# The neighbour sums of layer 3 as seven products of half matrices

## The chip, the cores and the metric

The kernel runs on one core of a Trainium2 chip. The core has five engines with a queue each: TensorE (PE in the profile, with its weight loads as PEld), VectorE (DVE), ScalarE (ACT), GpSimd (POOL) and SyncE (SP, which issues most DMAs here). Each queue is worked off in order. The metric is the device time of one execution in microseconds (us), lower is better. It is given as the median of a few runs.

## The reference

A stack of four graph layers over 16 graphs (batches) of 1024 nodes with 256 features each. The change lies in the last layer alone. With `h` the normalised and rectified input of one batch (1024 x 256) and `adj` its 1024 x 1024 adjacency matrix, layer 3 computes:

```python
h = jnp.maximum(_layernorm(x, axis=-1), 0.0)
neighbor_sum = jnp.einsum('bnm,bmd->bnd', adjacency, h)
agg = epsilon * h + neighbor_sum
h = jnp.einsum('bnd,dh->bnh', agg, W1) + b1        # 256 -> 1024
h = jax.nn.silu(_rmsnorm(h, rms_weight))
out = jnp.einsum('bnh,hd->bnd', h, W2) + b2        # 1024 -> 256
x = x + out
```

Everything is fp32. The first three layers, which take the first 3340 us or so of the execution, stay as they are.

## The kernel before

Layer 3 (`layer_3`, from L1093) works through the batches one after another. Matrices lie with 128 rows on the partitions, so `h[b]` is a tile of 8 row blocks by 256 columns, and the transposed adjacency of a batch is held as two halves, `at[b][0]` and `at[b][1]`, each of 8 row blocks by 512 output nodes. The epsilon term is folded in by adding `epsilon` to the diagonal blocks of `at` on GpSimd (`diagonal`, L1151).

One pass of the main loop (L1321) for batch b consists of:

- `load(b + 2)`: DMAs on SyncE for `x`, `hn` (what becomes `h`) and the two halves of `at`. Three halves fit at a time: two in a tile named `bxt`, one in `at`.
- `inner(b)`: `agg` times `W1`, written as seven products of half matrices (Strassen's scheme in Winograd's form) for each of four blocks k of 128 hidden features. Each product is one 128x128 by 128x512 matmul into a PSUM tile named `ph`, of which there are five (`bufs=5`). Per block, ScalarE copies the first product to `p1`; VectorE forms `u2` from the second and `p1`, `u3` from the third and `u2`, and four results `hh` (L1214). ScalarE squares each result into a tile `sq` (L1216), of which there are two, and GpSimd adds it into `ss` (L1218). The last result of a block is put off until after the next block's first product (`left`).
- `sums(b + 1)`: the neighbour sums of the next batch, in four parts, one for each half of the nodes and each half of the features. A part is eight matmuls of 128x128 by 128x512 that accumulate into one `ph`. ScalarE copies each part to `ag`, and four VectorE subtractions (L1195 to L1199) make the combinations `tt` that the next `inner` needs.
- `norm`: `mean` (after part 0) transposes `ss` on TensorE, reduces it on VectorE and takes the power -1/2 on GpSimd; `spread` (after part 1) transposes the result back. Then VectorE multiplies each of 16 tiles of `hh` by it (L1261) and ScalarE applies SiLU (L1262).
- `outer(b)`: `hh` times `W2`, again as seven products, each of 16 matmuls of 128x128 by 128x128 into PSUM tiles named `po`. VectorE makes combinations of `hh` in place (`combine`, L1273), one of them in the tile `s1`.
- `prepare(b + 2)`, called inside `outer` and queued on VectorE behind the update of `x21`: `x + hn`, statistics, the power -1/2 on GpSimd, `shift` (L1171), eight ReLUs on ScalarE that write `h` (L1173), and four GpSimd additions of `b2` (L1177).
- the output DMA, issued from GpSimd (L1337).

The order on each queue isn't the order of the code. It is fixed when the kernel is built, by a planner that goes through its own estimate of the durations and, whenever an engine is free, takes the ready instruction that stands first in the code. Work of later passes is moved forward into gaps in this way. On the chip the queues then run strictly in the order so fixed, whatever the real durations are.

In the profile, an fp32 matmul of the code appears as two MATMUL records, so one part of `sums` shows as 16 records and one product of `inner` as two.

Of the kernel before, what the change touches and what calls it, by code (L numbers as in the profile page):

```python
# [9 lines left out]
F32 = mybir.dt.float32  # L10
AF = mybir.ActivationFunctionType
ALU = mybir.AluOpType
# [4 lines left out]
P = 128  # L17
B, N, D, H = 16, 1024, 256, 1024
NT = N // P
DC = D // P  # L20
# [20 lines left out]
def gnn_stack(ctx: ExitStack, tc: tile.TileContext, a: dict, out: bass.AP):  # L41
    nc = tc.nc
# [29 lines left out]
    def rows(ap):  # L72
        return ap.rearrange("(t p) d -> p t d", p=P)
# [1019 lines left out]
    def layer_3(shared, x, hn, at, h, eye):  # L1093
        with ExitStack() as st:
            wp = st.enter_context(tc.tile_pool(name="w3", bufs=1))
            big = st.enter_context(tc.tile_pool(name="big3", bufs=2))
            small = st.enter_context(tc.tile_pool(name="small3", bufs=2))
            psum = st.enter_context(tc.tile_pool(name="psum3", bufs=2, space=PSUM))
# [14 lines left out]
            NH = 512  # L1113
# [3 lines left out]
            a11, a12, a21, a22 = (w1[:, c, p * HH * P : (p + 1) * HH * P] for p in range(2) for c in range(2))  # L1117
            nc.gpsimd.tensor_tensor(ws[:, 0], a21, a22, ALU.add)
            nc.gpsimd.tensor_tensor(ws[:, 1], ws[:, 0], a11, ALU.subtract)
            nc.gpsimd.tensor_tensor(a21, a11, a21, ALU.subtract)  # L1120
            nc.gpsimd.tensor_tensor(ws[:, 2], a12, ws[:, 1], ALU.subtract)

            wt = wp.tile([P, 3, HH, P], F32, name="wt")
# [6 lines left out]
            def load(b):  # L1130
                if b:
                    x[b] = big.tile([P, NT, D], F32, name="x", bufs=3)
                    nc.sync.dma_start(x[b], rows(x2_d[b]))
                    hn[b] = shared.tile([P, NT, D], F32, name="hb")
                    nc.sync.dma_start(hn[b][:, : NT - 1], rows(hn_d[b])[:, : NT - 1])
                    nc.sync.dma_start(hn[b][:, NT - 1], hs_d[NT - 1][b // GB][b % GB * P : (b % GB + 1) * P])
                    at[b] = []
                while len(at[b]) < N // NH:
                    n0 = NH * len(at[b])

                    if (2 * b + len(at[b])) % 3 < 2:
# [35 lines left out]
                    nc.gpsimd.tensor_tensor(to[:, t : t + 2], x[b][:, t : t + 2], b2[:, None].to_broadcast([P, 2, D]), ALU.add)  # L1177
                x[b] = to

            def sums(b):  # L1180

                ag = big.tile([P, DC, N], F32, name="ag", bufs=1)
                tt = big.tile([P, 4, NH], F32, name="tt", bufs=1)
                b21 = []

                def part(n0, c):
                    pa = psum.tile([P, NH], F32, name="ph", bufs=5)
                    for mt in range(NT):
                        nc.tensor.matmul(pa, h[b][:, mt, c * P : (c + 1) * P], at[b][n0 // NH][:, mt],  # L1189
                                         start=mt == 0, stop=mt == NT - 1)  # L1190
                    nc.scalar.copy(ag[:, c, n0 : n0 + NH], pa)
                    if (n0, c) == (0, 1):
                        b21.append(pa)
                    if (n0, c) == (NH, 0):
                        nc.vector.tensor_sub(tt[:, 0], pa, ag[:, 0, :NH])  # L1195
                    if (n0, c) == (NH, 1):
                        nc.vector.tensor_sub(tt[:, 1], pa, tt[:, 0])
                        nc.vector.tensor_sub(tt[:, 2], pa, ag[:, 0, NH:])
                        nc.vector.tensor_sub(tt[:, 3], b21[0], tt[:, 1])  # L1199
                return (ag, tt), [lambda n0=n0, c=c: part(n0, c) for n0 in range(0, N, NH) for c in range(DC)]  # L1200

            def inner(ag, tt):

                hh = [big.tile([P, HC, NH], F32, name=f"hh{q}", bufs=1) for q in range(2)]
                ss = [small.tile([P, NH], F32, name=f"ss{q}", bufs=1) for q in range(2)]
                begun = [False, False]

                def product(lhsT, rhs, onto=None):
                    ph = onto if onto is not None else psum.tile([P, NH], F32, name="ph", bufs=5)
                    nc.tensor.matmul(ph, lhsT, rhs, start=onto is None, stop=True, skip_group_check=onto is not None)  # L1210
                    return ph

                def result(k, q, ph, u):
                    nc.vector.scalar_tensor_tensor(hh[q][:, k], ph, b1[:, k : k + 1], u, op0=ALU.add, op1=ALU.add)  # L1214
                    sq = small.tile([P, NH], F32, name="sq") if begun[q] else ss[q]
                    nc.scalar.activation(sq, hh[q][:, k], AF.Square)  # L1216
                    if begun[q]:
                        nc.gpsimd.tensor_tensor(ss[q], ss[q], sq, ALU.add)  # L1218
                    begun[q] = True

                left = lambda: None
                for k in range(HH):
                    mine = slice(k * P, (k + 1) * P)
                    p1, u2, u3 = (small.tile([P, NH], F32, name=name) for name in ("p1", "u2", "u3"))
                    ph = product(a11[:, mine], ag[:, 0, :NH])
                    nc.scalar.copy(p1, ph)
                    left()
                    ph = product(ws[:, 1, mine], tt[:, 1])
                    nc.vector.tensor_add(u2, ph, p1)
                    ph = product(a21[:, mine], tt[:, 2])  # L1230
                    nc.vector.tensor_add(u3, ph, u2)
                    p5 = product(ws[:, 0, mine], tt[:, 0])
                    result(HH + k, 1, p5, u3)
                    result(HH + k, 0, product(a22[:, mine], tt[:, 3]), u3)
                    result(k, 0, product(a12[:, mine], ag[:, 1, :NH]), p1)
                    left = lambda k=k, mine=mine, p5=p5, u2=u2: result(
                        k, 1, product(ws[:, 2, mine], ag[:, 1, NH:], p5), u2)
                left()
                return hh, ss

            def norm(hh, ss):

                got = {}

                def mean():
                    all_ = small.tile([P, N // P], F32, name="all")
                    for q in range(2):
                        pq = psum.tile([P, NH // P, P], F32, name="po", bufs=3)
                        for n in range(NH // P):
                            nc.tensor.transpose(pq[:, n], ss[q][:, n * P : (n + 1) * P], ident)  # L1250
# [12 lines left out]
                return mean, spread  # L1263
# [50 lines left out]
            load(0)  # L1314
            prepare(0)
            load(1)
            ags, parts = sums(0)
            for part in parts:
                part()
            prepare(1)  # L1320
            for b in range(B):  # L1321
                if b + 2 < B:
                    load(b + 2)
                hh, ss = inner(*ags)
                mean, spread = norm(hh, ss)
                parts = [lambda: None] * 4
                if b + 1 < B:
                    ags, parts = sums(b + 1)
                parts[0]()
                mean()  # L1330
                parts[1]()
                spread()
                parts[2]()
                parts[3]()

                outer(b, hh, (lambda: prepare(b + 2)) if b + 2 < B else (lambda: None))
                nc.gpsimd.dma_start(rows(out[b]), x[b])  # L1337

    layers_0_1()
    with tc.tile_pool(name="shared", bufs=2) as shared:  # L1340
        x, hn, at, h = {}, {}, {}, {}
# [49 lines left out]
```

## Time and profile before

| what | us |
|---|---|
| runs shown | 4623.85, 4627.27, 4629.18 |
| median | 4627.27 |
| span of the profiled execution | 4622.5 |
| one pass of the main loop of layer 3 (from one `inner` to the next) | 78.31 |
| of it `inner` | 24.04 |
| the two first parts of `sums` with `mean` and `spread`'s transposes | 15.48 |
| the two last parts of `sums` | 13.73 |
| `outer` | 25.06 |

The profile gives the span from the first to the last instruction, and no time of its own beyond it; the median of the runs is 4.8 us above the span. The stage times are from the chain of waits for one pass in the steady part, the one that starts at 3924.34 us. Group rows of the profile list, for each line, engine and operation: the count, the busy time in us with the mean of one instruction in ns, and the idle time of the engine before them with what ended it.

### The profile page before, as it was taken

What the parts mean: (1) busy time and instruction counts of PE and PEld (TensorE: products, weight loads), DVE (VectorE), ACT (ScalarE), POOL (GpSimd) and SP (SyncE); (2) the same over time, 40 slices, a digit from 0 to 9 for tenths busy, and PEclk for the clock granted to TensorE, in tenths of its full rate; (3) what the DMA queues carried; (4) which work ended last, traced back from release to release, by engine and by line L of the source; (5) the groups of instructions that cost most, each with busy time, mean ns of one, the idle gap of its engine ahead of it and who ended that gap; (6) DMA issues with size and microseconds to landing.
All of it is one profiled execution on the core that took longest, in us unless ns stands there. A gap on an engine that the chain in (4) does not pass through costs nothing. (4 is left out here: it accounts for less than half of the span.)

```text
span 4622.5 us, 54868 instructions
## 1 busy us (share of the span) xinstructions
PE 4336.9 (94%) x19223; PEld 2956.2 (64%) x19223; DVE 2535.5 (55%) x6436; ACT 1279.5 (28%) x2741; POOL 1623.5 (35%) x1914
## 2 busy tenths in 40 slices
PE   8999799999997899999999999999799999999998
PEld 4444345555554687778787878787655656565656
DVE  6667944555554344444444444445356666676765
ACT  1111111221121232323232323233234333333333
POOL 3222333433333333332332323234244444445352
PEclk9999899999998999999999999999899999999999
DMA  4333244455544644454444454542142222232310
GB/s 150 112 116 100 73 112 146 164 194 188 156 145 154 196 138 154 131 166 141 154 121 151 131 159 135 167 144 73 55 142 89 100 92 92 88 104 82 110 46 19
DMA packets 530989, 576.78 MB, mean 125 GB/s; under 512 B 42544, under 2 KB 439472, under 8 KB 528304
## 3 DMA queue, kind: packets, MB, share of 16 engines
q1 hardware_dynamic: 499536, 460.27, 32.0%
q0 software_dynamic: 31040, 111.44, 6.9%
q8 instruction: 206, 3.38, 0.3%
q14 instruction: 207, 1.70, 0.1%
HBM read 469.65 MB, written 116.65 MB: 127 GB/s over the span
## 5 line engine op out<-in xcount | busy, mean ns | idle before, releaser
L295 PE MATMUL pa<-at,h 128*128 128x512 f32 x1088 | 495.3, 608 | 33.0 <-DVE ag L300 33.0
L295 PE MATMUL pa<-at,q 128*128 128x512 f32 x960 | 423.6, 594 | 0.0
L623 PE MATMUL pf<-hb,ab 128*128 128x256 f32 x1568 | 407.9, 383 | 14.5 <-DMA hb<-hs_d 5.7
L295 PEld LDWEIGHTS pa<-at,h 128*128 128x128 f32 x1088 | 209.7, 196 | 277.6 <-issue 231.5
L735 PE MATMUL pf<-hs,wx 128*128 128x256 f32 x1536 | 348.9, 381 | 19.2 <-POOL hs L726 17.6
L735 PEld LDWEIGHTS pf<-hs,wx 128*128 128x128 f32 x1536 | 290.6, 191 | 62.5 <-POOL hs L726 19.4
L623 PEld LDWEIGHTS pf<-hb,ab 128*128 128x128 f32 x1568 | 280.3, 191 | 67.2 <-issue 14.2
L295 PEld LDWEIGHTS pa<-at,q 128*128 128x128 f32 x960 | 178.2, 190 | 215.9 <-issue 212.8
L1189 PE MATMUL ph<-bxt,hb 128*128 128x512 f32 x704 | 310.8, 597 | 3.8 <-ACT hb L1173 3.0
L1218 POOL TENSOR_TENSOR ss<-ss,sq 128x512 f32<-128x512 f32 x224 | 280.7, 1271 | 87.1 <-ACT sq L1216 83.4
L1023 POOL DMA_INDIRECT hs_d<-h,table x128 | 129.6, 1013 | 330.0 <-ACTq L1009 150.8
L1279 PEld LDWEIGHTS po<-w,hh 128*128 128x128 f32 x2048 | 235.9, 193 | 9.5 <-issue 7.2
L1279 PE MATMUL po<-w,hh 128*128 128x128 f32 x2048 | 240.1, 277 | 1.4 <-ACT hh L1262 0.7
L1189 PEld LDWEIGHTS ph<-bxt,hb 128*128 128x128 f32 x704 | 133.2, 192 | 164.7 <-issue 159.8
L740 DVE TENSOR_TENSOR gates<-pf,bias 128x512 f32<-128x512 f32 x128 | 88.3, 691 | 238.6 <-PE pf L735 238.6
L1261 DVE TENSOR_TENSOR hh<-hh,po 128x512 f32<-128x512 f32 x256 | 154.5, 681 | 96.7 <-PE po L1258 96.7
L83 POOL TENSOR_TENSOR rs<-rs_v,mhalf 128x8 f32<-128x8 f32 (+1 forms) x65 | 106.9, 1645 | 255.0 <-DVE rs_v L79 241.5
L771 PE MATMUL pf<-bd,h 128*128 128x384 f32 (+4 forms) x512 | 185.6, 454 | 5.3 <-ACT bs L610 2.8
L1216 ACT ACTIVATE sq<-hh 128x512 f32<-128x512 f32 x224 | 141.1, 630 | 164.3 <-DVE hh L1214 125.6
L830 ACT ACTIVATE r<-pr 128x256 f32<-128x256 f32 (+3 forms) x230 | 68.1, 348 | 403.5 <-PE pr L789 389.5
L1214 DVE SCALAR_TENSOR_TENSOR hh<-ph,b,u 128x512 f32<-128x512 f32 x192 | 144.0, 751 | 64.9 <-PE ph L1210 54.8
L774 DVE TENSOR_TENSOR bxt<-bxt,pf 128x384 f32<-128x384 f32 (+4 forms) x256 | 125.0, 501 | 97.0 <-PE pf L771 95.5
(296 smaller groups left out, 8473.1 us busy)
## 6 DMA issues: line engine op xcount, KB each, us to landing
at<-in_adjT SPq DMA_DIRECT2D x64, 1024.0 KB, 7.1
ab<-in_adj SPq DMA_DIRECT2D x128, 512.0 KB, 4.3
bxt<-in_adjT SPq DMA_DIRECT2D x88, 512.0 KB, 6.7
at<-in_adjT SPq DMA_DIRECT2D x40, 512.0 KB, 6.8
ad<-in_adj SPq DMA_DIRECT2D x128, 128.0 KB, 6.2
x_d<-x POOLq DMA_DIRECT2D x16, 1024.0 KB, 5.1
he_d<-h POOLq DMA_DIRECT2D x16, 1024.0 KB, 8.9
heT_d<-hT POOLq DMA_DIRECT2D x16, 1024.0 KB, 4.2
```

Of the source, the lines that this page charges most:

```text
L295: nc.tensor.matmul(pa, h[:, mt, c * P : (c + 1) * P], at[n0 // 512][:, mt], start=mt == 0, stop=mt == NT - 1)
L623: nc.tensor.matmul(pb, ab[:, jts[k]], hb[:, jts[k]], start=k == 0, stop=k == len(jts) - 1)
L735: nc.tensor.matmul(pg[:, e], wx[:, c, q * D + e * P : q * D + (e + 1) * P], self.hs[:, c], start=c == 0, stop=c == DC - 1)
L771: nc.tensor.matmul(pf, h[:, g, c * P : (c + 1) * P], bd[:, g, b0 : b0 + n, S : S + far], start=True, stop=True)
L774: return lambda: nc.vector.tensor_add(to, to, pf)
L1023: nc.gpsimd.indirect_dma_start(out=hs_d[t][g][:, :], out_offset=row(1, g, t, s), in_=h[:, g], in_offset=None)
L1189: nc.tensor.matmul(pa, h[b][:, mt, c * P : (c + 1) * P], at[b][n0 // NH][:, mt], start=mt == 0, stop=mt == NT - 1)
L1214: nc.vector.scalar_tensor_tensor(hh[q][:, k], ph, b1[:, k : k + 1], u, op0=ALU.add, op1=ALU.add)
L1216: nc.scalar.activation(sq, hh[q][:, k], AF.Square)
L1218: nc.gpsimd.tensor_tensor(ss[q], ss[q], sq, ALU.add)
L1261: nc.vector.tensor_mul(hh[q][:, k], hh[q][:, k], pr)
L1279: nc.tensor.matmul(po[:, n], left[:, c, n * P : (n + 1) * P], right[:, c], start=onto is None and n == 0 and c == 0, stop=c == HH - 1, ski ...
```

## The change

The neighbour sums get the same seven-product scheme. The four quarters of the transposed adjacency are called `b11`, `b12`, `b21`, `b22` (the first index is the half of the input nodes, the second the half of the output nodes), and `m0`, `m1` are the halves of `h` by input nodes, each with two halves by features.

- `combined(b)`, new, called before `inner`: GpSimd makes four combinations of `h`, three in a new tile `hs` and one in place. VectorE's part comes back as two calls, `t1 = b11 + b12` (in place of `b12`) and `t2 = t1 + b22` (in a tile that shares the one buffer of `s1`). `inner` calls them in its blocks 1 and 2 (`between`). Each is two instructions of 128x1024.
- `sums(b)`: seven products of four matmuls each in place of four parts of eight. `first` makes products pa and p5, `second` p6 and a second product onto pa, `third` p7 and another, `fourth` one more onto p7. VectorE changes `t1` and `t2` in place between them (two instructions each). The outputs `ag` and `tt` are formed from the products by ScalarE copies and VectorE additions; one of the weights' combinations (L1120) changes its sign to go with them.
- The first batch runs `adds + parts` before the loop.

```diff
-            nc.gpsimd.tensor_tensor(a21, a11, a21, ALU.subtract)
+            nc.gpsimd.tensor_tensor(a21, a21, a11, ALU.subtract)
...
-            def sums(b):
+            def quarters(b):
+                left, right = at[b]
+                return left[:, : NT // 2], right[:, : NT // 2], left[:, NT // 2 :], right[:, NT // 2 :]
+
+            def add(engine, to, left, right, op):
+                for k in range(0, NT // 2, 2):
+                    two = slice(k, k + 2)
+                    engine.tensor_tensor(to[:, two], left[:, two], right[:, two], op)
+
+            def combined(b):
+
+                b11, b12, _, b22 = quarters(b)
+                m0, m1 = h[b][:, : NT // 2], h[b][:, NT // 2 :]
+                hs = big.tile([P, 3, NT // 2, P], F32, name="hs", bufs=1)
+                nc.gpsimd.tensor_tensor(hs[:, 0], m0[:, :, P:], m1[:, :, P:], ALU.subtract)
+                nc.gpsimd.tensor_tensor(hs[:, 1], hs[:, 0], m0[:, :, :P], ALU.subtract)
+                nc.gpsimd.tensor_tensor(m0[:, :, P:], m0[:, :, :P], m0[:, :, P:], ALU.subtract)
+                nc.gpsimd.tensor_tensor(hs[:, 2], m1[:, :, :P], hs[:, 1], ALU.add)
+                t2 = big.tile([P, NT // 2, NH], F32, name="s1", bufs=1)
+                return (t2, hs), [lambda: add(nc.vector, b12, b11, b12, ALU.add),
+                                  lambda: add(nc.vector, t2, b12, b22, ALU.add)]
+
+            def sums(b, t2, hs):
...
+                def product(left, right, onto=None):
+                    pa = onto if onto is not None else psum.tile([P, NH], F32, name="ph", bufs=5)
+                    for k in range(NT // 2):
+                        nc.tensor.matmul(pa, left[:, k], right[:, k], start=onto is None and k == 0, stop=k == NT // 2 - 1,
+                                         skip_group_check=True)
+                    return pa
...
+                def first():
+                    got["pa"] = product(m0[:, :, :P], b11)
+                    got["p1"] = room("p1")
+                    nc.scalar.copy(got["p1"], got["pa"])
+                    got["p5"] = product(hs[:, 0], t1)
+                    add(nc.vector, t1, t2, b11, ALU.subtract)
+
+                def second():
+                    p6 = product(hs[:, 1], t2)
+                    got["u2"] = room("u2")
+                    nc.vector.tensor_add(got["u2"], p6, got["p1"])
+                    add(nc.vector, t2, t2, b21, ALU.add)
+                    product(m1[:, :, :P], b21, got["pa"])
+                    nc.scalar.copy(ag[:, 0, :NH], got["pa"])
+
+                def third():
+                    p7 = product(m0[:, :, P:], t1)
+                    got["u3"] = room("u3")
+                    nc.vector.tensor_add(got["u3"], p7, got["u2"])
+                    nc.vector.tensor_sub(ag[:, 1, NH:], got["p5"], got["u3"])
+                    pa = product(m1[:, :, P:], t2)
+                    nc.vector.tensor_add(ag[:, 1, :NH], pa, got["u3"])
+                    got["p7"] = p7
+
+                def fourth():
+                    p7 = got["p7"]
+                    product(hs[:, 2], b22, p7)
+                    nc.scalar.copy(tt[:, 2], p7)
+                    nc.vector.tensor_sub(tt[:, 1], ag[:, 0, :NH], p7)
+                    nc.vector.tensor_sub(tt[:, 0], ag[:, 1, NH:], tt[:, 1])
+                    nc.vector.tensor_sub(tt[:, 3], ag[:, 1, :NH], tt[:, 1])
+                return (ag, tt), [first, second, third, fourth]
...
+                    if k and between:
+                        between.pop(0)()
...
-                hh, ss = inner(*ags)
+                adds = []
+                if b + 1 < B:
+                    of, adds = combined(b + 1)
+                hh, ss = inner(*ags, adds)
...
-                    ags, parts = sums(b + 1)
+                    ags, parts = sums(b + 1, *of)
```

More of the change, by code (lines that the diff above doesn't have):

```diff
@@ L1182, in sums @@
+            def sums(b, t2, hs):
                 ag = big.tile([P, DC, N], F32, name="ag", bufs=1)
                 tt = big.tile([P, 4, NH], F32, name="tt", bufs=1)
[L1184 to L1199, printed above, removed]
@@ L1200, in sums @@
-                return (ag, tt), [lambda n0=n0, c=c: part(n0, c) for n0 in range(0, N, NH) for c in range(DC)]
-            def inner(ag, tt):
+                b11, t1, b21, b22 = quarters(b)
+                m0, m1 = h[b][:, : NT // 2], h[b][:, NT // 2 :]
+                got = {}
+                def product(left, right, onto=None):
[4 more added lines that the diff above has]
+                    return pa
@@ new lines, in room @@
+                def room(name):
+                    return small.tile([P, NH], F32, name=name)
+                def first():
[11 more added lines that the diff above has]
+                    nc.scalar.copy(ag[:, 0, :NH], got["pa"])
@@ L1204, in inner @@
+                return (ag, tt), [first, second, third, fourth]
+            def inner(ag, tt, between):
                 hh = [big.tile([P, HC, NH], F32, name=f"hh{q}", bufs=1) for q in range(2)]
@@ L1316, in layer_3 @@
             load(1)
-            ags, parts = sums(0)
-            for part in parts:
+            of, adds = combined(0)
+            ags, parts = sums(0, *of)
+            for part in adds + parts:
                 part()
```

## The prediction

> **What bounds the kernel now.** I read the page's shares first, then a table by stage for one steady pass of layer 3, then the queues of GpSimd, VectorE and ScalarE in that pass.
>
> ```profile
> PE 4336.9 (94%) x19223; PEld 2956.2 (64%) x19223; DVE 2535.5 (55%) x6436; ACT 1279.5 (28%) x2741; POOL 1623.5 (35%) x1914
> ...
> PEclk9999899999998999999999999999899999999999
> ```
>
> Engine busy shares, and the TensorE clock granted in 40 slices. Layer 3 (from about 3340 us) has a nearly full clock.
>
> ```profile
> 3924.34:3948.38 24.04, 24.04 (x57) 10.65 (x57) 17.49 (x24) 10.83 (x18) 18.76 (x16) 1.00 0.27 88
> 3948.38:3963.86 15.48, 15.48 (x49) 7.73 (x49) 2.61 (x5) 2.43 (x4) 5.73 (x5) 1.00 0.01 1
> 3963.86:3977.59 13.73, 13.73 (x34) 6.08 (x34) 13.73 (x21) 10.39 (x17) 1.76 (x4) 1.00 0.44 153
> 3977.59:4002.65 25.06, 25.06 (x226) 25.06 (x225) 17.76 (x35) 5.22 (x10) 8.10 (x9) 1.00 0.36 127
> ```
>
> The stages of one pass: `inner`; two parts of `sums` with `mean`; two more parts; `outer`. Columns: length, then busy us of PE, PEld, DVE, ACT, POOL. TensorE is busy in all of each, so the pass of 78.31 us is TensorE's own work: fewer matmuls shorten it as long as no other engine holds TensorE up. The second thing to see is in the fifth number: GpSimd has 18.76 of 24.04 us in `inner`.
>
> ```profile
> 3907.18 3.54 POOL L1154 TENSOR_TENSOR bxt<-bxt,eye 128x128 f32<-128x128 f32 x4 [13.29 <-DMA bxt<-in_adjT]
> ...
> 3906.96 1.23 DVE L1273 TENSOR_TENSOR hh<-hh 128x1024 f32<-128x1024 f32 x1 [2.15 <-PE po L1279]
> ...
> 3918.85 1.26 POOL L1307 TENSOR_TENSOR x<-x,u 128x512 f32<-128x512 f32 x1
> ...
> 3918.90 1.23 DVE L1171 SCALAR_TENSOR_TENSOR shift<-mv,rs 128x8 f32<-128x8 f32 x1 [0.98 <-POOL rs L83]
> ```
>
> Four diagonal additions on GpSimd took 3.54 us; elsewhere one takes 0.46. The VectorE addition of 128x1024 that was running when they began shows who held them. Below, `shift`, an instruction of 128x8, took 1.23 us, while `rs_v` of that size takes 0.17: it began just after a GpSimd addition of 1.26 us and ended with it. Neither engine gets on while the other holds what they share.
>
> ```profile
> 3927.49 1.26 POOL L1177 TENSOR_TENSOR x<-x,b 128x512 f32<-128x512 f32 x1
> 3928.71 0.93 POOL L1337 DMA_DIRECT2D out<-x  x1
> 3931.09 1.26 POOL L1218 TENSOR_TENSOR ss<-ss,sq 128x512 f32<-128x512 f32 x1 [1.46 <-ACT sq L1216]
> 3932.74 1.27 POOL L1218 TENSOR_TENSOR ss<-ss,sq 128x512 f32<-128x512 f32 x1 [0.38 <-ACT sq L1216]
> 3935.44 5.08 POOL L1218 TENSOR_TENSOR ss<-ss,sq 128x512 f32<-128x512 f32 x4 [1.43 <-ACT sq L1216]
> 3941.45 5.09 POOL L1218 TENSOR_TENSOR ss<-ss,sq 128x512 f32<-128x512 f32 x4 [0.93 <-ACT sq L1216]
> 3947.46 5.08 POOL L1218 TENSOR_TENSOR ss<-ss,sq 128x512 f32<-128x512 f32 x4 [0.92 <-ACT sq L1216]
> ```
>
> GpSimd's queue around `inner` (which starts at 3924.34): after the output DMA it waits 1.46 us for the first square, and then has 0.38, 1.43, 0.93 and 0.92 us free up to 3952.54.
>
> ```profile
> 3935.53 0.63 ACT L1216 ACTIVATE sq<-hh 128x512 f32<-128x512 f32 x1 [0.23 <-DVE hh L1214]
> 3936.75 0.63 ACT L1216 ACTIVATE sq<-hh 128x512 f32<-128x512 f32 x1 [0.59 <-POOL ss L1218]
> 3937.28 0.57 ACT L1226 COPY p<-ph 128x512 f32<-128x512 f32 x1
> ```
>
> ScalarE in the same stage: the second of these squares waited 0.59 us for GpSimd to free a `sq`, and the copy to `p1` for block 2 stands behind it in the queue.
>
> **What the Trainium skill says.** "SBUF — State Buffer", section Who interferes with whom: a VectorE instruction with two SBUF inputs contends with a GpSimd instruction that reads SBUF, and whoever comes second blocks fully; with one SBUF input there is no contention. The trace agrees (the 3.54 and 1.23 us above), and the 224 `ss` additions, beside VectorE work that has a PSUM input, keep 1.27 us. "TensorE: Matmul & The Clock Gate", section What's actually happening: after an idle window of some 3.4 us the clock falls to a half until the next busy one. This trace agrees: where TensorE waited 4.78 us for `tt` at 3370, and 2.98 us for `ss` near 4577, half clock follows for 6.8 and 13.7 us.
>
> **The change, part by part.** Times are from the group rows unless a stage is named.
>
> *TensorE.* A `sums` pass costs 6.87 + 6.87 + 13.73 = 27.47 us for 64 records; 56 remain, 24.04 us. That saves 3.43 us in each of 15 steady passes, 51.5 us. The first batch, before the loop, is costed apart.
>
> *VectorE, in `sums`.* Two in-place combinations, four instructions of 1.22 us (row L1273), fall into the 15.48 us in which VectorE works 2.6: hidden. They delay `mean`'s reductions by up to 1.4 us; the transposes of `spread` come 6 us later, so that costs nothing. If this cover were gone, 4.9 us would be added. The steps at the end are six in place of four (`u3`, two parts of `ag`, three of `tt`), at 0.61 each in sequence: 1.2 more. Before, VectorE has 0.62 + 2.15 us idle in `outer`, waiting for `po`; this is used up. So VectorE gets to `prepare` (3910.69 now, 25.5 after the start of `spread`'s multiplications) 1.6 us earlier, while TensorE is 3.4 earlier: `shift`, the ReLUs and GpSimd's tail come 1.8 us later against `inner`.
>
> *The wait for `u3`.* `fourth` accumulates onto p7, which `u3` must have read. `u3` is queued behind the 16 multiplications (9.66 us); TensorE ends `third` 7.1 us after they start, so `fourth` can't start for another 3.2. The planner fills such gaps (it put eight matmuls of the next `outer` product into one now), and `outer`'s first product of 3.6 us is ready. I take 0; 3.2 if it isn't put there. Nothing below 0, as nothing is removed.
>
> *GpSimd.* The four combinations for `hs` are 4 x 1.265 = 5.1 us (row L1309, same size). They need the last ReLU, so they go in just before the first `ss` addition of `inner`, after the output DMA.
>
> *VectorE's `t1` and `t2` additions*, 4 x 1.22 us with both inputs in SBUF. They are ready once the right half has landed (the diagonals end 3910.7), come after `prepare` in the code's order, and so go to the gaps at the end of `outer` and in the first block of `inner`: there GpSimd has additions one after another. Each takes 1.22 us from GpSimd at worst, nothing if it meets GpSimd idle: 0 to 4.9 us. I take 3.0, since GpSimd works there without a gap from 3921.34 to 3929.64. VectorE itself loses some 0.6 us for each, which `inner`'s gaps (24.04 - 17.49 over four blocks, 1.6 us each) take up.
>
> *What follows for the first `ss` addition.* Later against `inner` by 5.1 + 3.0 + 1.8 - 1.5 (the idle time before it) = 8.4 us; bounds 5.4 and 10.3. It then starts 6.75 + 8.4 = 15.15 us into `inner`. The third `sq` after it waits for the third addition, which ends 15.15 + 3.8 = 18.95; square and copy follow, so `p1` of block 2 is there at 20.05, 6.6 us late. TensorE runs on: five products of that block fill the five `ph`, and the sixth, due at 16.3, waits for the copy: 3.8 us. The seventh waits 0.25 for VectorE. Block 3 has the same queue but lies later already: little is added. `inner` ends near 28.1 in place of 24.04: about 4.1 us lost, that is, the delay less 4.3. From 5.4 that makes 1.1, from 10.3 it makes 6.0. The `ss` additions end at 15.15 + 17.8 = 32.95, before TensorE needs them (35.0): no second loss. As the wait of 3.8 is near what has cost the clock above, I add 1.0 (between 0 and 1.7, half of a 3.4 us window).
>
> Sum: -3.43 + 4.1 + 1.0 = +1.7 us a pass, +25 us in 15.
>
> *The first batch.* Before, `sums(0)` begins at 3334.9 and TensorE runs `inner` without a gap from 3376.6. After, p5 needs `hs`, which GpSimd makes behind the weights and the `b2` additions, at 3357.2 + 1.3. From 3358.5 come p5, p6, p7 and the other two, 5 x 3.43, and `tt`: 3376.5 against 3374.75 for the first product that needs `tt`. With half clock after the wait I take +4 (-1 to +9). DMAs are the same in number and size; SyncE's releases of the halves move by less than a pass.
>
> Total: +29 on the span of 4622.5, which is 4651.5; the median of runs lay 4.8 above, so 4656.
>
> **The rivals.**
>
> 1. *The cover holds* (faster). Place: the first `ss` addition in `inner`. If the additions meet GpSimd idle, its delay is 5.4 us or less, TensorE loses 1.1 and no clock: -2.3 x 15 + 4 = -31, 4597; with no loss at all -47, 4580. The sign turns at a delay of 7.7 us (7.7 - 4.3 = 3.43). For it: VectorE has 2.95 us free at the end of `outer`, and GpSimd idles 1.23 before the `b2` additions. Against: the same stretch is where GpSimd is fullest. Chance 0.28.
> 2. *`fourth` waits.* 3.2 us at the end of `sums`; then GpSimd is less late against `inner` (5 to 6.6 us), which costs 1 to 2.3 there: -3.43 + 3.2 + 1.7 = +1.5 x 15 + 4, 4654. For it: order is fixed by estimates. Against: the eight matmuls put forward. Chance 0.12.
> 3. *The loss runs up.* Delay 10.3, 6.0 lost, clock 1.7: +4.3 x 15 + 8 = +72, 4699. For it: two engines blocking each other delay the results that feed `sq`. Chance 0.15.
>
> The forecast has 0.45. The seven products are there for all to count, so that the change doesn't do what it says is left out.
>
> **How the numbers follow.** A measurement of this kernel tells 0.2% (9 us) from no change. Faster: 0.26, from rival 1 save its edge. Same: 0.08, the edges of rival 1 and of the forecast. Slower: 0.66. The range, 4598 to 4700, leaves out half of rival 1 and the far end of rival 3. The forecast's own range is 4630 to 4680.
>
> **What would show it.** 896 records for the products of `sums`, 24.0 us a pass. First `ss` addition some 15 us into `inner` (6.75 now). ScalarE's `p1` copies waiting behind squares that wait for GpSimd. TensorE idle before the sixth product of blocks 2 and 3, with half clock here and there. Wrong, if `inner` stays at 24 to 25 us; if TensorE's idle time is named for `u3` or for `ss` at `mean`; or if the combinations are found elsewhere than at the end of `outer` and the head of `inner`.

## The result, and the profile after

| | before | after |
|---|---|---|
| median of four runs each | 4626.27 us | 4691.19 us |
| ratio, 95% interval | | 1.0143 [1.0126, 1.0161] |
| span of the profiled execution | 4622.5 us | 4688.3 us |
| first `inner` begins | 3368.95 | 3371.22 |
| from the first `inner` to the second | 85.36 | 96.84 |
| each of the 14 passes that follow, mean | 78.31 | 82.01 |
| of it `inner` (first to last product) | 24.20 | 31.38 |
| of it the rest | 54.11 | 50.63 |

The change makes the kernel slower, as forecast, by 65.8 us of span where 29 were forecast. The stretch outside `inner` is 3.48 us shorter (3.43 forecast): the seven products give what they promise. `inner` gives back 7.18. Fourteen passes of +3.70 make 51.8 us, the start and the first pass 13.7; nothing else of weight is left. `inner` is counted here from the start of its first product to the end of its last; the stages of before, in the section ahead of the prediction, begin 0.16 us later.

The shares of the engines on the page of the changed kernel, and the granted clock:

```profile
PE 4319.2 (92%) x19095; PEld 2931.5 (63%) x19095; DVE 2721.9 (58%) x6612; ACT 1268.3 (27%) x2725; POOL 1800.3 (38%) x1978
...
PEclk9999899999998999999999999999799999999999
```

128 matmuls are gone, and GpSimd has 177 us of work more. The stages of one pass, with the columns of the table shown of before (length; busy PE, PEld, DVE, ACT, POOL; clock; DMA):

```profile
3878.34:3909.54 31.20, 25.37 (x58) 10.23 (x57) 22.58 (x29) 14.28 (x26) 28.92 (x23) 1.00 0.21 68
3909.54:3925.00 15.46, 15.46 (x49) 7.70 (x48) 8.00 (x11) 2.80 (x5) 7.46 (x5) 1.00 0.00 0
3925.00:3935.30 10.30, 10.30 (x49) 6.47 (x48) 10.30 (x18) 9.79 (x16) 1.74 (x4) 1.00 0.73 248
3935.30:3960.34 25.04, 25.04 (x203) 23.13 (x203) 22.01 (x39) 1.30 (x3) 8.28 (x6) 1.00 0.31 109
```

Before, `inner` was full of TensorE and GpSimd had 18.76 us in it. Now TensorE idles 5.8 us there and GpSimd works 28.92 of 31.20. In the other three stages TensorE still has no gap: no time is lost at `mean`, and none to the wait for `u3`.

The end of `outer` and the head of the same `inner`, from the timeline (start, length, engine, line; in brackets the idle time before, and what ended it):

```profile
3874.52 0.16 DVE L79 TENSOR_SCALAR rs_v<-mv 128x8 f32<-128x8 f32 x1
3874.59 1.21 DVE L1187 TENSOR_TENSOR bxt<-at,bxt 128x1024 f32<-128x1024 f32 x1
3874.68 2.26 POOL L1360 TENSOR_TENSOR x<-x,u 128x512 f32<-128x512 f32 x1 [8.50 <-DVE rs_v L79]
3876.90 1.65 POOL L83 TENSOR_TENSOR rs<-rs_v,mhalf 128x8 f32<-128x8 f32 x1
...
3878.58 0.17 DVE L1171 SCALAR_TENSOR_TENSOR shift<-mv,rs 128x8 f32<-128x8 f32 x1 [2.78 <-POOL rs L83]
...
3878.79 4.04 ACT L1173 ACTIVATE hb<-x,shift,rs 128x256 f32<-128x256 f32 x8 [20.65 <-DVE shift L1171]
...
3880.41 4.50 DVE L1187 TENSOR_TENSOR s<-bxt 128x1024 f32<-128x1024 f32 x2
...
3881.58 2.25 POOL L1363 TENSOR_TENSOR x<-x,u 128x512 f32<-128x512 f32 x1
...
3886.16 1.12 PE L1261 MATMUL ph<-ag,w 128*128 128x512 f32 x2 [1.68 <-DVE u L1280]
```

A `t1` addition that takes 1.21 us costs the GpSimd addition beside it a full microsecond (2.26 against 1.26 before), and two `t2` additions take 4.50 us for 2.44. `shift` comes 0.24 us after the start of `inner`; before it came 5.28 us ahead of it. ScalarE's eight activations therefore lie in front of the first block's copy `p1`, VectorE's additions in front of its `u2`, and TensorE stops for both.

Further on in the same `inner`:

```profile
3894.32 1.27 POOL L1197 TENSOR_TENSOR hs<-hb,hs 128x512 f32<-128x512 f32 x1
...
3895.55 7.62 POOL L1269 TENSOR_TENSOR ss<-ss,sq 128x512 f32<-128x512 f32 x6
...
3896.85 0.63 ACT L1267 ACTIVATE sq<-hh 128x512 f32<-128x512 f32 x1 [6.11 <-POOL ss L1269]
...
3899.94 0.57 ACT L1277 COPY p<-ph 128x512 f32<-128x512 f32 x1
...
3900.56 1.12 PE L1261 MATMUL ph<-tt,w 128*128 128x512 f32 x2 [3.04 <-ACT p L1277]
...
3901.52 1.88 PE L1261 MATMUL ph<-ag,w 128*128 128x512 f32 x4
```

This is the forecast's chain, link by link: `hs` ahead of the first addition to `ss`, the squares waiting for it, the copy `p1` of block 2 queued behind the squares, TensorE waiting for the copy. The first `ss` addition starts 17.2 us into `inner`; 15.15 were forecast. One link is a product off: TensorE stops at the fifth product of block 2, behind 36 records, where the forecast had the sixth, behind 38.

### The profile page after: what moved, and what is told of

It is laid out like the page before. It is cut to its first block, busy times and chain, and to the rows that moved or that the text cites. A ratio compares the mean times of both kernels' runs of the same rounds, so it can differ in the third digit from the quotient of the medians.

```text
span 4688.3 us, 54984 instructions
## 1 busy us (share of the span) xinstructions
PE 4319.2 (92%) x19095; PEld 2931.5 (63%) x19095; DVE 2721.9 (58%) x6612; ACT 1268.3 (27%) x2725; POOL 1800.3 (38%) x1978
## 3 DMA queue, kind: packets, MB, share of 16 engines
q1 hardware_dynamic: 499536, 460.27, 31.7%
q8 instruction: 205, 3.36, 0.3%
## 5 line engine op out<-in xcount | busy, mean ns | idle before, releaser
L300 DVE COPY ag<-pa 128x512 f32<-128x512 f32 x64 | 44.0, 687 | 244.5 <-PE pa L295 244.3
L1261 PE MATMUL ph<-tt,w 128*128 128x512 f32 x256 | 134.9, 609 | 40.1 <-ACT p L1277 39.7
L847 DVE TENSOR_TENSOR w<-w,hc 128x256 f32<-128x256 f32 (+3 forms) x230 | 87.8, 382 | 137.5 <-ACT hc L846 137.5
L601 POOL TENSOR_SCALAR_AFFINE_SELECT ab<-ab 128x128 f32<-128x128 f32 x112 | 34.4, 307 | 342.9 <-DMA ab<-in_adj 274.8
```

## The experiments

Theory A, at the start: GpSimd's lateness, by `hs` and by blocking, is the loss. Rivals: VectorE's additions at the head of `inner`; the new place of the addition to `x12` ahead of the power. "Pass" is the mean of the 14 passes from the second `inner` to the last, in the profiled execution. Runs 1 to 5, 11 and 12 were timed once each, so their readings rest on these passes. Every group of runs has runs of before from its own chip; their medians lie between 4620 and 4626 us.

**1. A third tile for the squares.**

```diff
-sq = small.tile([P, NH], F32, name="sq") if begun[q] else ss[q]
+sq = small.tile([P, NH], F32, name="sq", bufs=3) if begun[q] else ss[q]
```

> Three tiles for the squares in place of two, nothing else. Theory A (GpSimd's additions to ss run late; the squares wait for them on ScalarE's queue, and the copy to p1 stands behind the squares): the copy for block 2 has to wait for one addition fewer, 1.27 us earlier, so the longest wait of TensorE in the matmuls of W1 (3.0 us in the changed kernel) falls to about 1.8, a pass from 82.0 to 80.7 us and the whole by some 18 us. Rival B (VectorE's own additions to t1 and t2 hold up its later work, GpSimd's lateness costs nothing): no difference over 3 us. Rival C (the halves of the adjacency land too late): no difference.

4664.7 us, a pass of 80.30, `inner` 29.66. TensorE's wait in block 2 falls from 3.04 to 1.72 us in the pass looked at, or less in others. The queue of squares is a part of the way, and one tile buys 1.7 us a pass, some 26 us in all where 18 were expected.

**2. Without `hs`.**

```diff
-                hs = big.tile([P, 3, NT // 2, P], F32, name="hs", bufs=1)
-                nc.gpsimd.tensor_tensor(hs[:, 0], m0[:, :, P:], m1[:, :, P:], ALU.subtract)
...
+                hs = None
```

> The four GpSimd combinations of h are left out, and the products read plain quarters of h in their place; TensorE's and VectorE's work is the same. Theory A: GpSimd's first addition to ss starts 5.1 us earlier, 12 us into the stage; the wait of 3 to 4 us in block 2 goes, the 3.4 us lost in block 0 stay; a pass of 78.4 us, the whole about 50 us below the changed kernel, 4640. Rival B: unchanged, 4690. Rival C: unchanged.

4629.4 us, a pass of 78.41, as theory A had it; rivals B and C, which allowed no change, are out. Block 2's wait is gone, but `inner` is 27.78, not 24.2: some 3.6 us remain, all of it in the first ten products.

**3. Without the early additions of adj.**

```diff
-                return (t2, hs), [lambda: add(nc.vector, b12, b11, b12, ALU.add),
-                                  lambda: add(nc.vector, t2, b12, b22, ALU.add)]
+                return (t2, hs), []
...
-                    add(nc.vector, t1, t2, b11, ALU.subtract)
+                    add(nc.vector, t1, b22, b11, ALU.subtract)
...
-                    add(nc.vector, t2, t2, b21, ALU.add)
+                    add(nc.vector, t2, b22, b21, ALU.add)
```

> VectorE's early additions b11 + b12 and t1 + b22 are left out, and the products and later combinations read b12 and b22 in their place. Theory A: block 0 loses nothing any more (3.4 us), and GpSimd is not held for 3.8 us, so the wait in block 2 falls from 3.7 to about 1.5 to 2: a pass of 76.6, the whole about 4610. Rival B: all of the 7.2 us go, a pass of 74.9 and 4585. Rival C: unchanged, 4690.

4674.15 us, a pass of 81.35: a miss by 64 us. The trace shows why it could not settle anything:

```profile
3946.01 1.21 DVE L1187 TENSOR_TENSOR s<-at,bxt 128x1024 f32<-128x1024 f32 x1
3946.10 2.26 POOL L1359 TENSOR_TENSOR x<-x,u 128x512 f32<-128x512 f32 x1 [8.50 <-DVE rs_v L79]
3948.32 1.65 POOL L83 TENSOR_TENSOR rs<-rs_v,mhalf 128x8 f32<-128x8 f32 x1
```

Once `t2` no longer came from the early sum, the late addition b22 + b21 waited for no product, and the planner moved its two halves to the very place from which the early ones had been taken. The addition to `x12` was blocked as before. Run 12 repeats it cleanly.

**4. The addition to `x12` behind the power.**

```diff
+                with tc.issue_after(powers[-1].ins):
+                    nc.gpsimd.tensor_tensor(x12, x12, u2, ALU.add)
```

> GpSimd's addition to x12 is queued behind the power -1/2 of the next batch's statistics, as in the kernel before; all work is the same. Theory A: shift and the ReLUs come about 2 us earlier against TensorE, the first addition to ss 1.7 us earlier, and the wait in block 2 falls from 3.7 to about 2: a pass of 80.2, the whole about 4663. Rival B and C: unchanged within 3 us.

4693.84 us, a pass of 82.10: no gain, another miss. The order did change:

```profile
3877.01 1.21 DVE L1189 TENSOR_TENSOR bxt<-at,bxt 128x1024 f32<-128x1024 f32 x1
3877.17 2.57 POOL L85 TENSOR_TENSOR rs<-rs_v,mhalf 128x8 f32<-128x8 f32 x1 [8.58 <-DVE rs_v L81]
3879.71 1.26 POOL L1363 TENSOR_TENSOR x<-x,u 128x512 f32<-128x512 f32 x1
3879.77 1.23 DVE L1173 SCALAR_TENSOR_TENSOR shift<-mv,rs 128x8 f32<-128x8 f32 x1 [1.55 <-POOL rs L85]
```

Now VectorE's addition blocks the power (2.57 for 1.65), and the addition to `x12`, which follows, blocks `shift` (1.23 for 0.17). Whoever goes first, the three stand in line for the same thing; this change of order on one engine moved the blocking and didn't remove it.

**5. The products alone (first try).** Runs 2 and 3 together.

> Left out: both kinds of additions. hs isn't built (its three products read plain quarters of h) and no combination of adj is formed (t1, t2 are plain quarters, and the two written in place before the third product are a single difference and a single sum each). So it is the seven products and their three sums of results alone. Theory D, from the four runs before: three delays, of hs on GpSimd, of the additions on VectorE and of the statistics, lie over one another. The statistics of the product after next begin only after outer's x21, and VectorE reaches them some 3.4 us later against the start of inner than before, because TensorE's stretch between mean and inner is shorter by 3.48 us while VectorE's chain in it (normalizing, combinations, statistics) is not. So ScalarE's eight activations still run into inner, and its copy p1 of the first block is queued behind them: a pass of 75.5 to 77 us, inner 25 to 26.5 us, time 4585 to 4605. Rival (hs and the additions are the whole loss): inner as before, 24.1 us, a pass of 74.8 us, time 4565 to 4578.

4586.9 us, a pass of 75.93, `inner` 25.30. In the band of theory D, but not clean: the two moved additions of run 3 are in it too.

**6. `prepare` earlier.**

```diff
                 mean()
+                if b + 2 < B:
+                    with tc.issue_after(done[-1].ins):
+                        prepare(b + 2, roots[-1])
+                    with tc.issue_after(powers[-2].ins):
+                        rest(b + 2)
                 parts[1]()
...
-                outer(b, hh, (lambda: prepare(b + 2)) if b + 2 < B else (lambda: None))
+                if b + 2 < B:
+                    hs = halves(b + 2)
+                outer(b, hh, lambda: None)
+                if b + 2 < B:
+                    of, adds = combined(b + 2, hs)
+                    for part in adds:
+                        part()
```

`done` holds the results of `inner`, `rest` the second half of the diagonal and the sums of b2, `halves` the four combinations of h.

> The whole computation. prepare of the product after next (statistics, power, activations) moves from behind outer's x21 to VectorE's idle stretch behind inner's last result, hs is built on GpSimd right behind the fourth product, before outer, with the sums of b2 on GpSimd behind the power of the mean, and the early additions of adj are queued behind outer's combinations. Theory D: nothing of GpSimd's tail but x12, x21, x22 is left in inner, ScalarE's activations and VectorE's additions are out of its head; inner 24 to 24.6 us, the rest of a pass 50.6 to 51.3, a pass of 74.8 to 75.8 us; time 4568 to 4590, faster than both. Rival (VectorE has no room in that stretch: statistics 6.7 us, additions 4.9, reductions 1.4 between two ends 15 us apart, so mean and the normalizing come late): inner 24.2, the rest 53 to 54, a pass of 77.5 to 78.5; time 4605 to 4630.

4643.24 us, 1.0042 [1.0025, 1.0059]. Half of it held: `inner` is back at 24.20 in every pass. But the rest took 54.01, a pass of 78.21, so these numbers are the rival's; the time is above both bands, as the first pass took 102.4 us (85.36 before). VectorE's multiplications of the normalizing began 17.8 us after the end of `inner` (15.1 before), ScalarE's eight activations stood in front of its sixteen of the normalizing, and `outer` waited for these:

```profile
3996.23 1.10 PE L1343 MATMUL po<-wt,hh 128*128 128x128 f32 x4 [2.35 <-ACT hh L1326]
```

**7. The same move in the kernel before.**

> The kernel before with prepare moved in the same way, the sums as eight products as they were. Theory D: in the kernel before nothing of prepare ends late (the activations end 0.2 us into inner, the first addition of squares waits for nothing else), TensorE bounds inner and the rest, so the move brings nothing: 78.0 to 78.6 us a pass, 4618 to 4632. Rival (the move would be a gain of its own, and what the sixth run gains has nothing to do with the seven products): below 4610.

4623.72 us, 1.0000 [0.9991, 1.0008], a pass of 78.31. Moving `prepare` is worth nothing in the kernel before, so it is fair to compare run 10 below with that.

**8. The activations behind the normalizing.**

```diff
+                    with tc.issue_after(silus[-1].ins):
+                        activate()
                     hs = halves(b + 2)
+                    rest(b + 2)
```

> The whole computation: the sixth run with one thing changed. There inner was back at 24.20 us, but the rest of a pass took 54.01 instead of 50.63: ScalarE's eight activations of prepare (4 us, from 37.9 us before the next inner) stood in front of the sixteen of the normalizing, which began 2 us late, and outer's first product waited for them. Here they are queued behind the sixteen, and the sums of b2, which overwrite their input, behind them. Theory D: inner stays at 24.2, the rest goes to 50.6 to 51.2, a pass of 74.8 to 75.4; time 4590 to 4605. Rival (VectorE is the bound of that stretch, and the normalizing is late because the multiplications are): the rest stays over 53, time 4630 to 4645.

4671.67 us, 1.0103 [1.0086, 1.0120]: a miss, and slower than run 6. `inner` is 24.20, the rest 56.24, over 53 as the rival had it; the time is above both bands. VectorE and GpSimd in the middle of `outer`:

```profile
4015.40 2.29 DVE L1341 TENSOR_TENSOR hh<-hh,hh 128x1024 f32<-128x1024 f32 x1
...
4018.78 2.25 POOL L1205 TENSOR_TENSOR hs<-hb 128x512 f32<-128x512 f32 x1
...
4023.19 4.49 DVE L1341 TENSOR_TENSOR hh<-s,hh 128x1024 f32<-128x1024 f32 x2
...
4024.35 2.24 POOL L1207 TENSOR_TENSOR hb<-hb 128x512 f32<-128x512 f32 x1
...
4028.33 3.90 PE L1347 MATMUL po<-wt,hh 128*128 128x128 f32 x18 [2.36 <-DVE x L1365]
```

Pushed back by the activations, the sums of b2 now lie beside the combinations of `outer` too, as `hs` did in run 6. Each takes about a microsecond from the other, and TensorE waits for VectorE.

**9. The first batch too.** Run 8, with the sums of b2 of product 0 ahead of W2's combinations, and `prepare` of product 1 behind the first sums' last difference.

> The whole computation: the eighth run, and in the first batch the additions of b2 of product 0, which free the buffer of the next h, are queued ahead of the four combinations of W2, prepare of product 1 behind the last difference of the first sums on VectorE, and adj's additions for product 1 inside the first inner as in the changed kernel. The changed kernel's first batch came 13.7 us later than before's at the second inner, the sixth run's 18 us. Theory D (those queue positions hold the first batch): 8 to 14 us off the eighth run; 4578 to 4596. Rival (the first batch is late because hs and the combinations of adj come between the last tile of h and the first product, whatever is behind them): within 4 us of the eighth run.

4679.48 us, 1.0117 [1.0098, 1.0135], no better than run 8, so theory D is out. TensorE's wait for `tt` in the first `inner` fell from 9.93 us (run 8) to 3.84, but a wait for a copy `p1` in the same `inner` grew from 3.82 to 6.85.

**10. GpSimd's additions beside work that reads PSUM, and the statistics earlier.**

```diff
-                hs = big.tile([P, 3, NT // 2, P], F32, name="hs", bufs=1)
+                hs = [big.tile([P, NT // 2, P], F32, name=f"hs{k}", bufs=1) for k in range(3)]
...
                     with tc.issue_after(powers[-2].ins):
                         rest(b + 2)
+                        hs = halves(b + 2)
+                if b + 1 < B:
+                    with tc.issue_after(roots[-1].ins):
+                        parts[4]()
```

This is run 6 with three changes: `hs` is moved and split, `parts[4]`, the addition for the third product, is taken out of `first`, and the power of the statistics now comes ahead of that of the mean.

> The whole computation: the sixth run with three things changed, by what the eighth showed: GpSimd's additions took 1.27 us there while VectorE multiplied by a tile in PSUM, and VectorE's combinations took 2.29 instead of 1.22 us where GpSimd's additions lay beside them. (1) hs is three tiles, so that its first parts needn't wait for the fourth product, and hs stands on GpSimd behind the sums of b2, beside VectorE's sixteen multiplications; (2) the power of the statistics goes ahead of that of the mean; (3) adj's additions for the third product are queued behind the statistics. Theory E (what bounds the stretch behind inner is VectorE and GpSimd together[...]): ScalarE's eight activations end before the normalizing begins, the combinations take 1.2 to 1.3 us, inner 24.2, the rest 50.6 to 51.6, a pass of 74.8 to 75.8; time 4595 to 4612, faster than before. Rival (VectorE's own sum is the bound, without GpSimd): the rest stays at 53 to 54, time 4630 to 4645.

4593.56 us against 4624.35 on the same chip, 0.9931 [0.9915, 0.9948]: faster than both kernels, inside its band. The pass is 75.17, `inner` 24.20, the rest 50.97. From the timeline, during the normalizing and after:

```profile
3957.41 5.10 POOL L1186 TENSOR_TENSOR x<-x,b 128x512 f32<-128x512 f32 x4
...
3958.18 9.65 DVE L1329 TENSOR_TENSOR hh<-hh,po 128x512 f32<-128x512 f32 x16 [0.51 <-PE po L1326]
...
3962.47 1.28 POOL L1201 TENSOR_TENSOR hs<-hb 128x512 f32<-128x512 f32 x1
...
3963.83 1.28 POOL L1202 TENSOR_TENSOR hs<-hs,hb 128x512 f32<-128x512 f32 x1
...
3965.07 1.28 POOL L1203 TENSOR_TENSOR hb<-hb 128x512 f32<-128x512 f32 x1
...
3971.81 1.22 DVE L1341 TENSOR_TENSOR hh<-hh,hh 128x1024 f32<-128x1024 f32 x1
```

The same instructions as in run 8, at 1.28 and 1.22 us: beside a multiplication that reads `po` in PSUM, GpSimd and VectorE take nothing from each other. "SBUF — State Buffer", section Who interferes with whom, says as much of a VectorE instruction with one SBUF input, and runs 8 and 10 are the two sides of it. How the gain over run 6 divides among the three changes is not shown. TensorE's wait of 2.35 us in run 6 is gone because the multiplications begin 15.4 us after the end of `inner` and ScalarE's first of the sixteen 1.07 us after them (17.8 and 2.80 in run 6); all of this lies ahead of `hs`, so it speaks for the two changes of order. What the place of `hs` brought in time, no run separates.

**11 and 12. The products alone, and `hs` alone, cleanly.** In both, the addition that had moved in run 3 is queued behind `inner`'s last result; 11 is otherwise run 5, and 12 is run 3.

```diff
+                    with tc.issue_after(done[-1].ins):
+                        add(nc.vector, t2, b22, b21, ALU.add)
```

> Left out: hs and both kinds of early additions, as in the fifth run (its products read plain quarters, the two quarters written in place are a single difference and a single sum). The fifth run was not clean: with t2 made of b22 and b21 alone, two of the late additions no longer waited for a product, and the planner moved them to the end of outer and the head of inner, where the early ones had been. Here they are queued behind inner's last result. Theory D: what is left is the late statistics alone, ScalarE's activations end some 3 us into inner, the copy p1 of the first block is 1 to 2 us late, and the five tiles of PSUM hide most of that: inner 24.2 to 24.8, a pass of 74.8 to 75.4, time 4568 to 4582. Rival (the fifth run's 1.1 us in inner came from the late statistics, not from the two additions): a pass of 75.9, time 4585 to 4592.

4573.37 us, a pass of 74.95, `inner` 24.32. The products bring 3.36 us a pass when nothing stands against them, and late statistics alone cost 0.12: TensorE's five tiles of PSUM cover a first copy `p1` that ends 1.9 us later (3.55 us into `inner`, 1.65 before).

> Left out: the early additions, as in the third run, and the two late ones that had moved into their place there are queued behind inner's last result. So hs alone is added to the products. Theory D: without VectorE's additions beside it GpSimd's tail loses no time to blocking; from the power's end near -0.8 us against inner it has x21, x22, four sums of b2, hs and the output, 13.7 us, so the first addition of squares begins 12.5 to 13.5 us into inner (15.3 in the third run); a delay of 6 us less the 4.3 of the prediction's sum, and some 0.5 for the late copy: inner 26 to 27, a pass of 76.5 to 77.6, time 4605 to 4622. Rival (the third run's 6.5 us in inner are hs's own, the two additions in it did nothing): a pass of 81 us or more, 4660 to 4676.

4637.37 us, a pass of 78.72, `inner` 27.61: between the two theories. The first `ss` addition starts 13.2 us into `inner`, as expected:

```profile
4025.98 7.64 POOL L1274 TENSOR_TENSOR ss<-ss,sq 128x512 f32<-128x512 f32 x6
...
4030.38 0.57 ACT L1282 COPY p<-ph 128x512 f32<-128x512 f32 x1
...
4031.00 1.12 PE L1266 MATMUL ph<-tt,w 128*128 128x512 f32 x2 [2.25 <-ACT p L1282]
```

but this delay costs more than the forecast's rule gives, and another 0.48 us is lost outside `inner`, where in 12 of the passes `mean`'s transposes wait some 0.33 us for `ss`.

## Why the forecast had the direction right and the size wrong

The path was right, and with it the direction: runs 11 and 12 and the changed kernel add `hs` and then the early additions to the products, and `inner` goes from 24.32 to 27.61 to 31.38. The step that failed is the price of that path. The forecast had `hs`, blocking and the late start delay the first `ss` addition by 8.4 us, let TensorE cover 4.3 of them, and added 1.0 for the clock: 5.1 us of loss a pass. Measured are a delay of 10.2, a cover of 3.0 and nearly nothing for the clock: 7.18.

What the runs leave is one rule for `inner`. From the start of the first `ss` addition to the end of block 2's copy `p1` it is 4.96 us in the changed kernel (3895.55 to 3900.51) and 4.97 in run 12; over all 14 passes of these two and of runs 3 and 4 it is 4.95 to 4.97. TensorE, at one record in 0.4286 us, would come to the product that waits for the copy 36 x 0.4286 = 15.43 us into `inner`. A restart and the last products cost another 0.4. So the loss is the first `ss` start + 5.0 - 15.4 + 0.4, unless waits at the head cost more:

| kernel | first `ss`, us into `inner` | by the rule | `inner` less 24.20 |
|---|---|---|---|
| before | 6.93 | none | 0 |
| 11, products alone | 8.01 | none | 0.12 |
| 2, without `hs` | 11.90 | 1.9 | 3.58 (head) |
| 12, `hs` alone | 13.24 | 3.2 | 3.41 |
| 3 | 15.27 | 5.3 | 6.52 |
| 4 | 16.97 | 7.0 | 7.26 |
| after | 17.15 | 7.1 | 7.18 |

The rule was found on the changed kernel and run 12; run 1, where three tiles shorten the 4.96 to 3.62, tests it: 5.7 by the rule from a first `ss` at 17.13, 5.47 measured. Run 3 lies above it: in 12 of its 14 passes half clock (TensorE granted 0.5 of its clock) follows the wait, and in the other two `inner` loses about 5.0 and 5.4. Run 2 is the one where the head decides. In the changed kernel the head loses some 3.6 us as well, but that adds nothing: TensorE then comes later to block 2 and waits less there. Passes show it directly: in four of them half clock slows the products after the head by some 1.7 us, block 2's wait is 1.3 instead of 3.0, and `inner` takes 31.3 to 31.7 us either way.

By the steps of the forecast:

- *TensorE, -3.43 a pass*: right (-3.48, and -3.36 in run 11).
- *VectorE in `sums` hidden, and the wait for `u3` at 0*: right. TensorE has no gap there.
- *Late start of GpSimd's tail, 1.8, less 1.5 of idle time*: 0.3 net; run 11 shows 1.1 (6.93 to 8.01). VectorE reaches `rs_v` 2.9 us later against `inner` there (1.8 were forecast), and 3.3 in the changed kernel. In both, `u2` (0.65 us) stands ahead of `rs_v`, where the planner had put it behind before; in the changed kernel four combinations beside GpSimd's additions to the diagonal take 5.6 us for 4.9.
- *`hs`, 5.1*: right. From run 11 to run 12, 5.2.
- *`t1` and `t2` block GpSimd for 3.0*: 3.9 from run 12 to the changed kernel. Four GpSimd instructions (the additions to `x12`, `x21`, `x22`, the first sum of b2) lose about a microsecond each.
- *The loss is the delay less 4.3*: the term that was mis-sized most. By the rule above TensorE stands a delay of 3.1, as the product that has to wait is the fifth of block 2, due at 15.4, and not the sixth at 16.3, and the end of `inner` adds 0.3. With the measured delay of 10.2 the forecast's rule gives 5.9; 7.2 was lost.
- *Clock, 1.0*: nearly nothing. After the wait of 3.04 us above, two products (four records) take 1.88 us, as they do where nothing waits; where half clock does fall into the head, block 2's wait takes it up.
- *VectorE loses 0.6 for each addition, which gaps take up*: wrong by itself (3.6 us at the head in run 2, where these additions are in and `hs` is out), though of no weight in the total, as GpSimd is later still.

So three terms were short by 0.8, 0.9 and 1.3 us, and the clock was long by 1.0: 2.0 us a pass, 28 in the 14 passes. The start and the first pass were put at +4 and +1.7, and came to 13.7. There TensorE waits 9.79 us for `tt` (4.78 before) and 5.23 for a copy `p1`, and half clock follows both:

```profile
3374.21 0.69 DVE L1163 TENSOR_TENSOR x<-x,hb 128x512 f32<-128x512 f32 x1 [8.96 <-DMA hb<-hn_d]
...
3382.04 2.07 PE L1261 MATMUL ph<-tt,ws 128*128 128x512 f32 x2 [9.79 <-DVE tt L1248]
...
3383.91 1.91 PE L1261 MATMUL ph<-tt,w 128*128 128x512 f32 x2
...
3411.63 2.08 PE L1261 MATMUL ph<-tt,w 128*128 128x512 f32 x2 [5.23 <-ACT p L1277]
```

The forecast took the last product for the cause of `tt`. In the trace VectorE's `prepare` of product 1 stands in front of the differences that make `tt`, and waits 8.96 us for a load. Run 9 moved it, and the time did not fall, so what would bring the 13 us back stays open; run 10 has them still.

Rival 1 (the cover holds) gave 4580 for no loss at all; that is what run 11 shows, 4573, but only with `hs` and the early additions left out. Rival 3 (4699) named the delay that came, 10.3, and its total is 8 us off. That it is so near is luck in part: its 1.7 us a pass for the clock wasn't there, and makes up for a cover that was put too large.

## What to carry to other kernels

When a stage gets shorter on its busiest engine, ask of each other engine when its last piece of work for the next stage is done against the new start, and write that as a due time; a slack that is 1 us wrong counts once in every pass. Treat VectorE's additions with two inputs in SBUF and GpSimd's additions as one queue: here a GpSimd addition cost nothing beside VectorE work that reads PSUM (run 10), and a change of order on GpSimd alone only moved the blocking (run 4). In an experiment that takes work out, look where the planner puts what remains before reading the time.

## What the runs showed of the hardware

- Prices of blocking both ways, with no work lost or added: a GpSimd addition of 128x512 takes 1.27 us alone and 2.18 to 2.26 beside a VectorE addition of 128x1024; that one takes 1.22 alone and 2.25 to 2.29 beside GpSimd; GpSimd's power of 128x8 takes 1.65 and 2.57; `shift` of 128x8 takes 0.17 and 1.23.
- Half clock does not hang on the length of the last wait. In the 14 passes it never came after the waits of 1.3 to 3.1 us in block 2 of the changed kernel; it came in 12 after those of 3.3 us in run 3, in 2 after those of 2.25 us in run 12, and in 6 of the changed kernel and 6 of run 2 after short waits at the head (0.6 and 1.7 us; 0.24 and 1.69 us).
- The traces show what it goes with. The half-clock stretches of one trace begin on a grid with steps of 3.41 us (to within 4 ns), which can be laid over the whole of the part from 3385 to 4560 us. In the 14 traces together, all 65 steps at full clock in which TensorE's records leave more than 1.95 us idle are followed by half clock, none of the 4622 with less than 1.77, and 14 of the 28 between. So two short waits within one step cost the clock, and a wait of 3.0 us that falls on two steps (1.4 and 1.7 us idle, in the pass shown above) doesn't.
- "TensorE: Matmul & The Clock Gate", section What's actually happening, gives as the condition an idle window of some 3.4 us, free-running. The grid agrees with such a window, but a window that is a little over half idle was enough. The wait of 2.98 us that the prediction took for agreement shows the same: TensorE's last record before it ends at 4574.87, and half clock begins 2.05 us later.
